# A mixture-of-experts stage in two passes: all first products into one PSUM bank with one bias addition and one Gelu, then all products with the second weights

## The chip, the core and the metric

The kernel runs on one core of a Trainium2 chip. A core has five engines with queues of their own: TensorE (PE in the profile; PEld is its weight load) multiplies matrices and writes into PSUM, VectorE (DVE) and ScalarE (ACT) work on elements, GpSimd (POOL) here only issues gathers, and SyncE (SP) issues nearly all other DMAs. Each queue runs in order: an instruction that waits holds up everything behind it on its engine. PSUM has eight banks of 128 partitions by 512 fp32. The metric is the device time of one execution in microseconds (us), lower is better.

## The reference

Four images of 64 x 64 tokens with 128 channels pass through four layers: deformable attention (layer 0), linear attention (layer 1), an attention and a mixture of experts (layer 2), a causal linear attention and a spectral filter (layer 3). The change touches the experts alone. Cut to them:

```python
def _L2_ffn_ref(x, gate_w, gate_b, weight1, weight2):      # E = 64 experts, K = 8, H = 512, O = 128
    logits = jnp.einsum('bsd,ed->bse', x, gate_w) + gate_b
    probs = jax.nn.softmax(logits, axis=1)
    vals, idx = jax.lax.top_k(probs.transpose(0, 2, 1), K)
    ...
    pooled = jnp.einsum('bked,bke->bed', gathered, topv)
    ones = jnp.ones((E, Bn, 1), dtype=x.dtype)
    h = jnp.concatenate([pooled.transpose(1, 0, 2), ones], axis=-1)
    h = jax.nn.gelu(jnp.einsum('ebd,edh->ebh', h, weight1), approximate=False)
    h = jnp.concatenate([h, ones], axis=-1)
    out = jnp.einsum('ebh,eho->ebo', h, weight2)
    ...
```

For each image every expert gets one pooled token of 128 numbers, multiplies it with its own 128 x 512 matrix, adds a bias, applies Gelu, and multiplies with its own 512 x 128 matrix (the appended one is a second bias). So an image's experts are 64 vector-matrix products of each kind, and 2 x 64 x 256 KB = 33.5 MB of weights, read again for each image.

## The kernel before

All arithmetic is fp32. `hybrid` (line 1733) interleaves two programs. Image b's deformable attention (`Layer0.attend`, line 597) is a loop of 128 steps: four per 128 tokens, one for each of four groups. A step gathers nine samples by nine indirect DMAs on POOL into one of three buffers gt, multiplies them on VectorE with the query (lines 619 to 629), takes the exponential ex on ScalarE (line 633), and forms the weighted sum on VectorE (lines 637 to 645). Beside it run the first stages of image b+1 (`Layer0.front`: the tables from which samples are gathered, lines 428 to 479), and everything that follows for image b-1: `Post.run` (line 808), a generator through layers 1 to 3, of which `layer2_ffn` (line 1029) is one part. Each `yield` of it names a cost; after each attention step `hybrid` advances it until its costs have reached 1176 x (steps done) / 128. When the last image's attention is over, `Post.run` goes through once more alone, with more buffers (`self.wide`).

That is the order in which the program is written. The framework's planner then orders the instructions of each engine's queue itself, by that order as a priority and by when it believes that inputs and buffers are there; so a queue can hold more attention steps beside a stage than the costs say. A buffer of a pool is given again once the readers of its last tile are done.

The experts, in `layer2_ffn` from line 1102, go in 16 groups q of four experts (e = 16 j + q for j from 0 to 3). A group, in order:

- Lines 1112 to 1123: SP loads the four first matrices (w1) and the four second ones (w2), 256 KB each. A tile holds two matrices; the pool has three tiles of each kind beside attention, and ten of each kind in the last, wide run, where the pool is open from the start of `run` (line 811), so that loads can land early.
- Line 1126: four products of one row, ph, for the four experts at partitions 0, 32, 64 and 96 of one bank (one bank beside attention, two wide).
- Line 1131: ScalarE copies the bank to hs. Line 1135: four small products with a matrix that picks these four rows turn hs around into pt, 128 x 16: a hidden unit per partition.
- Line 1140: VectorE adds the bias, g. Line 1143: ScalarE applies Gelu.
- Line 1146: 16 products of g's columns with w2 sum the four experts' outputs into po. After each fourth group line 1153 copies po to os, and line 1156 stores it.

Gelu and the exponential need different tables in ScalarE; a change between them is a table load, an instruction of its own in the trace.

## Time and profile before

| | us |
|---|---|
| time, median of 3 runs (lowest to highest) | 9904.06 (9867.37 to 9940.72) |
| the profiled execution | 9948.3 |
| its span, first to last instruction | 9946.3 |
| attention of images 0 to 3, from about | 273 to 8686 |
| experts of images 0, 1 and 2, beside attention | 2537 to 2850, 4790 to 5096, 7031 to 7299 |
| experts of image 3, alone | 8954 to 9060 |
| mean granted TensorE clock | 0.762 of full speed |

The page of the profile gives, for each engine, its busy time and its instructions, and for each group of instructions the busy time, the mean duration of one, and the idle time of the engine just before it with what ended that. "DVE g L1140 <- PE pt L1135" reads: VectorE stood still before the instruction of line 1140 that writes g, until TensorE's instruction of line 1135 that writes pt was done. "Remote" is a wait whose end the profile can't tie to an instruction. The ends of matrix products are modelled, and some of their records are missing.

The expert stages are where rows of lines 1126 to 1156 stand. Three of the four are beside attention, so a row of theirs can wait for an engine that is busy with another image, and the reverse.

### The profile page before, as it was taken

How to read it: one execution, taken by the hardware profiler on the slowest of the kernel's cores; microseconds unless marked ns; L12 is line 12 of the kernel's file. 1: busy time of each engine (PE TensorE's matmuls, PEld its weight loads, DVE VectorE, ACT ScalarE, POOL GpSimd, SP SyncE). 2: the span in 40 equal slices, each digit the busy share in tenths (PEclk: the TensorE clock that was granted, in tenths of full speed). 3: DMA queues.
4: the chain of work that ended last, by engine and by line, in shares of the span. 5: the costliest groups of instructions: out<-in, count | busy, mean ns of one | idle time of the engine just before them, and what ended most of it. 6: DMA issues, size and time to landing. Idle time of an engine off the chain costs nothing.

```text
span 9946.3 us, 87181 instructions
## 1 busy us (share of the span) xinstructions
PE 5961.9 (60%) x30347; PEld 4144.4 (42%) x30347; DVE 4645.0 (47%) x7777; ACT 2263.7 (23%) x4192; POOL 4400.1 (44%) x4736
## 2 busy tenths in 40 slices
PE   7454100056675777756675667744455667757899
PEld 6242000034344555525344445522234455534676
DVE  1555555565455444466454344456454444443222
ACT  3100000023222222223222222213222222232222
POOL 0665666655434555454534445455535445400000
PEclk9677555567787888877787788866677888877999
DMA  6443333334644444345644444444645444344323
GB/s 211 140 129 109 105 101 105 101 105 142 185 138 142 118 119 121 106 137 150 186 142 141 107 110 119 115 133 140 186 124 147 113 108 116 110 138 127 106 70 81
DMA packets 1131344, 1263.41 MB, mean 127 GB/s; under 512 B 392990, under 2 KB 915481, under 8 KB 1126681
## 3 DMA queue, kind: packets, MB, share of 16 engines
q1 hardware_dynamic: 907309, 652.59, 23.8%
q0 software_dynamic: 221184, 604.27, 21.1%
q8 instruction: 240, 3.93, 0.2%
q14 instruction: 199, 1.63, 0.1%
q10 hardware_dynamic: 2412, 0.98, 0.0%
HBM read 1061.76 MB, written 195.61 MB: 126 GB/s over the span
## 4 chain that ended last, share of the span: by engine, by line
PE 23%; another core or an unknown queue 13%; issue 5%; ACT 5%; DVE 5%; DMA 3%; SPq 1%; POOL 0%; DVEq 0%; ACTq 0%
PE pa L1441 10%; PE pq L1417 4%; ACT y L1431 2%; DMA xin<-x 1%; PE ph L1126 1%; PE pm L428 1%; DVE o L645 1%; PE pt L744 1%; PE pq L874 0%; DVE pr L619 0%; PE pa L1237 0%; PE pn L1247 0%; PE po L1321 0%; PE pt L1135 0%
## 5 line engine op out<-in xcount | busy, mean ns | idle before, releaser
L610 POOL DMA_INDIRECT gt<-tbl,idx x4608 | 4391.2, 953 | 4225.3 <-DVE pv L642 2419.9
L1441 PE MATMUL pa<-y,m 128*128 128x256 f32 x8192 | 2147.1, 415 | 197.6 <-issue 168.1
L1441 PEld LDWEIGHTS pa<-y,m 128*128 128x128 f32 x8192 | 1647.1, 207 | 686.8 <-issue 427.1
L1431 ACT COPY y<-pq 128x1024 f32<-128x1024 f32 x896 | 869.6, 1015 | 2311.6 <-remote 1335.1
L637 DVE TENSOR_TENSOR qa<-cw,ex 128x36 f32<-128x36 f32 x512 | 104.5, 204 | 2212.4 <-ACT ex L633 2066.3
L1417 PE MATMUL pq<-th,xh 32*128 32x256 f32 x8192 | 715.8, 455 | 653.0 <-ACT y L1431 389.1
L645 DVE TENSOR_REDUCE o<-pv 128x32 f32<-128x1152 f32 x512 | 1075.4, 2100 | 21.5 <-remote 10.4
L428 PE MATMUL pm<-wd,xT 128*128 128x256 f32 x2376 | 643.5, 420 | 292.1 <-ACT kv L439 178.3
L1417 PEld LDWEIGHTS pq<-th,xh 32*128 32x128 f32 x8192 | 432.8, 210 | 864.7 <-ACT y L1431 430.6
L619 DVE TENSOR_TENSOR pr<-gt,qa 128x1152 f32<-128x1152 f32 x512 | 689.8, 1347 | 179.3 <-DMA gt<-tbl,idx 151.3
L642 DVE TENSOR_TENSOR pv<-gt,qa 128x1152 f32<-128x1152 f32 x512 | 691.7, 1351 | 70.0 <-remote 25.7
L624 DVE TENSOR_REDUCE s<-pr 128x36 f32<-128x1152 f32 x512 | 687.4, 1343 | 1.8 <-DVE sc L627 1.2
L428 PEld LDWEIGHTS pm<-wd,xT 128*128 128x128 f32 x2376 | 485.2, 211 | 421.8 <-ACT kv L439 198.2
L633 ACT ACTIVATE ex<-sc,mx 128x9 f32<-128x9 f32 x512 | 157.0, 307 | 1131.4 <-DVE mx L629 504.4
L461 PE MATMUL pm<-xT,wd 128*128 128x512 f32 x576 | 309.6, 686 | 171.7 <-ACT qo L478 125.5
L1428 DVE COPY y<-pq 128x1024 f32<-128x1024 f32 x128 | 156.8, 1225 | 466.2 <-ACT y L1431 466.2
L579 PE MATMUL qa<-sident,qt 128*128 128x128 f32 x256 | 52.0, 336 | 437.7 <-issue 266.5
L1126 PE MATMUL ph<-w,pooled 128*1 128x512 f32 x512 | 234.1, 800 | 47.9 <-DMA w<-in_L_ffn_weight_dram 30.5
L461 PEld LDWEIGHTS pm<-xT,wd 128*128 128x128 f32 x576 | 120.1, 220 | 336.8 <-issue 185.2
L661 PE MATMUL pt<-ident,o 128*128 128x128 f32 x128 | 33.5, 353 | 355.2 <-issue 253.9
L147 ACT ACTIVATE ln<-xin,ln,ln 128x128 f32<-128x128 f32 x512 | 212.3, 483 | 122.1 <-DMA xin<-x 88.6
L579 PEld LDWEIGHTS qa<-sident,qt 128*128 128x128 f32 x256 | 44.7, 235 | 454.2 <-issue 276.0
(377 smaller groups left out, 6399.4 us busy)
## 6 DMA issues: line engine op xcount, KB each, us to landing
w<-in_L_ffn_weight_dram SPq DMA_DIRECT2D x512, 256.0 KB
th<-th SPq DMA_DIRECT2D x512, 256.0 KB
gt<-tbl,idx POOLq DMA_INDIRECT x4608
xin<-x SPq DMA_DIRECT2D x224, 256.0 KB
x<-xin SPq DMA_DIRECT2D x160, 256.0 KB
tbl<-kv SPq DMA_DIRECT2D x264, 128.0 KB
th<-wx SPq DMA_DIRECT2D x32, 1024.0 KB
q<-qd SPq DMA_DIRECT2D x288, 64.0 KB
```

What stands on the lines that cost most here:

```text
L147: self.nc.scalar.activation(dst, src, AF.Identity, bias=self.shift[:, i : i + 1], scale=self.rstd[:, i : i + 1])
L428: nc.tensor.matmul(pm[:, t, :], lhsT=self.xf[:, at : at + P], rhs=self.wd[:, tap, C:], start=(t == 0 and tap == 0), stop=False,)
L461: nc.tensor.matmul(pv, lhsT=self.wd[:, tap, :C], rhs=self.xT[:, 8 * c + dy : 8 * c + dy + 8, dx : dx + HW], start=(tap == 0), stop=False,)
L610: nc.gpsimd.indirect_dma_start(out=gt[:, i, :], out_offset=None, in_=self.tbl[b % 2][:, :], in_offset=bass.IndirectOffsetOnAxis(ap=blk.idx ...
L619: nc.vector.tensor_mul(pr, corners[:, :, 0:32], qa[:, q0 + 32 * g : q0 + 32 * g + 32].unsqueeze(1).to_broadcast([P, 4 * K2, 32]),)
L624: nc.vector.tensor_reduce(s4, pr, AX.X, ALU.add)
L642: nc.vector.tensor_mul(pv, corners[:, :, 32:64], aw.unsqueeze(2).to_broadcast([P, 4 * K2, 32]),)
L645: nc.vector.tensor_reduce(o[:, t, 32 * g : 32 * g + 32], pv.rearrange("p i s -> p s i"), AX.X, ALU.add)
L1126: nc.tensor.matmul(ph[32 * j : 32 * j + 1, :], lhsT=pooled[:, 16 * j + q : 16 * j + q + 1], rhs=w1s[j], start=True, stop=True,)
L1417: nc.tensor.matmul(pq[:, r // 2, r % 2, :, pair, :], lhsT=xh[rows, 2 * (q % 4) + pair, :], rhs=t[rows, 2 * (q % 2) + pair, :].rearrange("p ...
L1431: nc.scalar.copy(to, src)
L1441: nc.tensor.matmul(pa[:, h * 2 * P : (h + 1) * 2 * P].rearrange("p (g x) -> p g x", g=8), lhsT=s.m[u][:, KC * kc + i, :], rhs=yv[:, i], st ...
```

## The change

The groups run in two passes. The first takes all 16 groups as far as pt, which becomes one tile for all of them: 16 columns a group, 256 in all, in one bank. Then one addition adds all biases, and one Gelu is applied. The second pass makes the products with the second weights, and copies and stores as before. Both kinds of weights come from tiles of one tag, w: six of them beside attention and 20 in the wide run, the same bytes as before. The copy os now uses the two buffers of hs. Each pass yields 2.5 sixteen times, where one loop yielded 5.0 sixteen times.

```diff
@@ run
-            self.ws = self.pool(ctx, "fwx", 10) if self.wide else None
+            self.ws = self.pool(ctx, "fwx", 20) if self.wide else None
@@ layer2_ffn
-                ws = self.ws or self.pool(ectx, "fws", 3)
+                ws = self.ws or self.pool(ectx, "fws", 6)
                 wk = self.pool(ectx, "few", 2)
...
+                pt = ps.tile([P, 512], F32, tag="p", name="pt")
+                ptv = pt[:, : 4 * E].rearrange("p (q c j) -> p q c j", c=4, j=4)
+
+                def first(e):
+                    return self.a["L2_ffn_weight1"][e, :C, :]
+
+                def second(e):
+                    return self.a["L2_ffn_weight2"][e, :FH, :].rearrange("(c p) o -> p c o", p=P)
+
+                def weights(q, src):
+
+                    got = []
+                    for j in range(4):
+                        if j % 2 == 0:
+                            t = ws.tile([P, 2, FH], F32, tag="w", name="w")
+                        to = t[:, j % 2]
+                        if src is second:
+                            to = to.rearrange("p (c o) -> p c o", c=4)
+                        nc.sync.dma_start(to, src(16 * j + q))
+                        got.append(t[:, j % 2])
+                    return got
+
                 for q in range(16):
-                    w1s, w2s = [], []
-                    for j in range(4):
-                        e = 16 * j + q
-                        if j % 2 == 0:
-                            w1 = ws.tile([P, 2, FH], F32, tag="w1", name="w1")
-                            w2 = ws.tile([P, 2, 4, C], F32, tag="w2", name="w2")
-                        nc.sync.dma_start(w1[:, j % 2], self.a["L2_ffn_weight1"][e, :C, :])
-                        nc.sync.dma_start(
-                            w2[:, j % 2],
-                            self.a["L2_ffn_weight2"][e, :FH, :].rearrange("(c p) o -> p c o", p=P),
-                        )
-                        w1s.append(w1[:, j % 2])
-                        w2s.append(w2[:, j % 2])
+                    w1s = weights(q, first)
                     ph = phs[q % len(phs)]
...
                     hs = wk.tile([P, FH], F32, tag="hs", name="hs")
                     nc.scalar.copy(hs, ph)
-                    pt = ps.tile([P, 512], F32, tag="p", name="pt")
-                    ptv = pt[:, :16].rearrange("p (c j) -> p c j", c=4)
                     for c in range(4):
                         nc.tensor.matmul(
-                            ptv[:, c, :], lhsT=hs[:, c * P : (c + 1) * P], rhs=w.pick,
+                            ptv[:, q, c, :], lhsT=hs[:, c * P : (c + 1) * P], rhs=w.pick,
                             start=True, stop=True,
                         )
-                    g = wk.tile([P, 4, 4], F32, tag="g", name="g")
-                    nc.vector.tensor_add(
-                        g, ptv, w.b1T.rearrange("p c (j q) -> p q c j", j=4)[:, q]
-                    )
-                    nc.scalar.activation(g, g, AF.Gelu)
+                    yield 2.5
+                g = wk.tile([P, 16, 4, 4], F32, tag="g", name="g", bufs=1)
+                nc.vector.tensor_add(g, ptv, w.b1T.rearrange("p c (j q) -> p q c j", j=4))
+                nc.scalar.activation(g, g, AF.Gelu)
+                for q in range(16):
+                    w2s = weights(q, second)
                     for c in range(4):
                         for j in range(4):
                             nc.tensor.matmul(
                                 po[32 * j : 32 * j + 1, (q % 4) * C : (q % 4 + 1) * C],
-                                lhsT=g[:, c, j : j + 1], rhs=w2s[j][:, c, :],
+                                lhsT=g[:, q, c, j : j + 1], rhs=w2s[j][:, c * C : (c + 1) * C],
                                 start=(c == 0), stop=(c == 3),
                             )
                     if q % 4 == 3:
-                        os = wk.tile([P, 4, C], F32, tag="os", name="os", bufs=1)
+                        os = wk.tile([P, 4, C], F32, tag="hs", name="os")
                         nc.scalar.copy(os.rearrange("p q c -> p (q c)"), po)
...
-                    yield 5.0
+                    yield 2.5
```

## The prediction

> **What bounds the kernel now.** I read the page first (busy times, then the chain of waits), then busy times by stretch, then the waits inside the three stretches in which image b's experts run beside image b+1's attention, then the order of time inside one of them.
>
> ```profile
> PE 5961.9 (60%) x30347; PEld 4144.4 (42%) x30347; DVE 4645.0 (47%) x7777; ACT 2263.7 (23%) x4192; POOL 4400.1 (44%) x4736
> ...
> PE 23%; another core or an unknown queue 13%; issue 5%; ACT 5%; DVE 5%; DMA 3%; SPq 1%; POOL 0%; DVEq 0%; ACTq 0%
> ```
>
> No engine is full: the kernel is bound by engines that wait for each other. The changed lines run four times. These stretches, in order, are attention beside little else (the yardstick), the three expert stages beside attention, and the last one alone ("wide"):
>
> ```profile
> core 0: us, PE busy (x) PEld busy (x) DVE busy (x) ACT busy (x) POOL busy (x), PEclk, DMA share, GB/s
> 1160.00:1960.00 800.00, 59.56 (x178) 37.04 (x178) 442.39 (x605) 37.78 (x153) 540.97 (x570) 0.52 0.35 103
> 2537.00:2850.00 313.00, 198.97 (x1051) 92.35 (x1050) 136.09 (x202) 67.53 (x122) 157.41 (x166) 0.77 0.62 190
> 4790.00:5096.00 306.00, 195.66 (x984) 86.54 (x985) 131.26 (x192) 58.21 (x109) 148.77 (x158) 0.74 0.61 187
> 7031.00:7299.00 268.00, 132.96 (x820) 55.18 (x819) 115.44 (x176) 55.31 (x100) 136.61 (x146) 0.66 0.66 203
> 8954.00:9060.00 106.00, 81.38 (x770) 38.74 (x769) 3.30 (x17) 17.95 (x39) 0.00 (x0) 0.73 0.73 219
> ```
>
> Counted by line 642 (one product per group of nine samples), the yardstick holds 63 attention steps in 800 us, 12.7 us each. The expert stages hold 19, 18 and 16 steps, which alone would take 241, 229 and 203 us. So the experts cost 72, 77 and 65 us more than the attention that they run beside: 214 us in all is the most that hiding them fully could save there. DMA is not full: its share makes 194, 187 and 177 us of busy time, under the attention's own time.
>
> Where the 214 us go, first stage:
>
> ```profile
> POOL gt L610 <- DVE pv L642: 119.8, 13, 18.0
> ACT hs L1131 <- remote: 92.4, 6, 23.4
> DVE g L1140 <- PE pt L1135: 84.6, 11, 19.1
> ...
> DVE g L1140 <- remote: 43.1, 3, 23.8
> DVE qa L637 <- ACT ex L633: 37.2, 10, 17.4
> ```
>
> and SP's own waits, between its DMA issues:
>
> ```profile
> SPq L1118 <- remote: 88.8, 4, 23.8
> SPq L1118 <- PE po L1146: 46.9, 7, 9.4
> ```
>
> VectorE stands still before the bias addition g (with short ones, 131, 118 and 112 us in the three stages) and ScalarE before the copy hs (121, 105, 105 us). Both carry attention too: what stands behind them waits, the gather buffers are not freed, and POOL stops. One of the long ones:
>
> ```profile
> 7243.01 1.05 PE L1126 MATMUL ph<-w,pooled 128*1 128x512 f32 x3 [0.22 <-issue]
> ...
> 7252.22 0.95 POOL L610 DMA_INDIRECT gt<-tbl,idx  x1 [0.30 <-issue]
> 7256.49 1.48 SPq L1118 DMA_DIRECT2D w<-in_L_ffn_weight_dram  x3
> 7256.70 0.59 ACT L1131 COPY hs<-ph 128x512 f32<-128x512 f32 x1 [16.14 <-remote]
> ...
> 7259.24 0.18 DVE L1140 TENSOR_TENSOR g<-pt,b1T 128x16 f32<-128x16 f32 x1 [13.84 <-PE pt L1135]
> ```
>
> The product ends at about 7244, yet its reader and SP's next load start at 7256.5, some 3.3 us after POOL's last gather. TensorE's word arrives late while POOL streams gathers ("remote" in these rows). So each handover from TensorE to an engine that attention needs can cost up to some 20 us.
>
> **The change, part by part.** Durations are of the profiled execution: 9948.3 us, its span of 9946.3 plus 2.0 around it. The median shown is 9904.06, 0.44% less; I carry the sum over as a ratio.
>
> *Removed: additions and Gelus.* Per stage 16 additions of 0.176 us and 16 Gelus of 0.216 become one of each on 256 columns. Nearest rows: line 1176 adds 512 columns in 0.69 us, line 1131 copies 512 in 0.59; so about 0.4 us each. The busy time saved, some 5 us a stage, lies beside waits: nothing counted. What counts is the wait: 16 handovers from TensorE to VectorE become one.
>
> *Removed: table loads.* Gelu and attention's Exp displace each other: 14, 12 and 12 loads before Gelu and 13, 12 and 12 before Exp, 75 of 1.283 us, 96 us of ScalarE. Those before Exp stand in VectorE's path (line 637 waits for ex); the others lie partly beside products. The Trainium skill, "ScalarE: Activation LUTs", section "What ACT_TABLE_LOAD costs", puts a switch at about 2.66 us, as it adds a drain to the load. In this trace Gelu starts 0.01 us after its load ends (7239.05 plus 1.28, Gelu at 7240.34), so I use 1.283: 37 loads before Exp are 47 us, by the page they would be 98.
>
> *Moved: second products, and their weights.* All 512 products with the second weights (rows of 0.27 to 0.42 us, four side by side) go behind the last first product. In pass two nothing of VectorE waits for an expert, and ScalarE only for four copies os. I give pass two half of the stage, so 107 of the 214 us, and let 85% go: 91 us. The rest stays for os and for TensorE's waits for weights.
>
> *Pass one.* It keeps its 16 copies hs, each waiting for TensorE, on the engine that also has to issue ex: what the additions no longer hold, these can hold. Of its 107 us I take off the Exp loads of its half, 24 us, and 20 more for the vanished additions. The ends are 0 (hs holds all that g held) and 80 (the waits of g go and none is replaced); I stay near the low end because hs waited 331 us in sum already, g 361, largely at the same time.
>
> *Added: the border.* The addition waits for the last of 16 groups, then Gelu, then the first second product. One ordinary handover is about 2 us; a held one, by the row at 7256, 16 us more. I take 8 us a stage, 24 in all. Meanwhile six tiles of second weights load, which covers the start of pass two. Here the Trainium skill speaks against the change: "Perfetto Trace Analysis", section "Matmuls" under "Optimizing Tensor Performance", wants independent products to rotate through PSUM banks so that reading one overlaps the next, and the change stops doing that for pt. By the rule the emptying is exposed; by the rows it is one addition of 0.4 us instead of 16 waits summing to over 110 us a stage. I follow the rows; the rule's cost is inside the 24.
>
> *Weights on SP.* Still 128 DMAs of 256 KB a stage at about 0.50 and 0.43 us of issue, 60 us; none added. They are reordered: 64 of the first kind, then 64 of the second, six shared tiles in place of three and three. A load now waits for the product three half-steps before, no longer for the second product at the end of the chain (SP waited 136 us for that in the first stage). Behind a waiting load on SP stand attention's query loads and the table stores of the next image: they gain with it. POOL's queue is passed by nothing. TensorE now meets a load's wait in both passes (7, 23 and 50 us in one today); with the same bytes I count no change, 0 to 15 us a stage either way. The copy os shares hs's two buffers in place of one of its own: nothing, as hs is idle then; without that cover, four waits of a 2 KB store, a few us.
>
> *The wide stage.* 106 us hold 81 us of TensorE and 0.73 x 106 = 77 us of DMA. TensorE idles 20 us before products of these lines. Without the round trip by ScalarE, VectorE and ScalarE in each group it should come to 81 plus some 12 at the two ends: 12 us off (0 to 25).
>
> Sum: 91 + 24 + 20 - 24 + 12 = 123 us; 9948.3 becomes 9825, a ratio of 0.9876, and the median 9904 becomes 9782. Nothing takes the gain back later: what follows on each queue just starts sooner.
>
> **Rivals.** *The wait moves to ScalarE.* Attention's ex queues behind hs. For it: hs already waits longest for "remote", and pass one meets twice as many copies per attention step. Against it: pass two has none. Then pass one loses more than before, pass two gives 91, and what is left is some 40 us: 9865, no change.
>
> *Fewer attention steps beside the experts (slower).* The planner fixes each queue's order. By pacing, a stage of cost 80 at 1176/128 = 9.19 a step should pass 8.7 attention steps; the trace has 16 to 19, because the chain of waits kept the experts behind. If the plan now sees a short chain, about 9 steps remain beside them. The stage is then DMA's: 33.5 MB at 219/0.73 = 300 GB/s is 112 us, gathers 9 x 0.35 x 12.7 = 40, other transfers some 15, so 167 us at a full share. Attention alone needs 114. At a share of 0.70 the stage takes 239 us, 125 over attention where it was 72: 160 us more in three stages, about 10050. It decides below a share of 0.76 (219 us); the stages have 0.61 to 0.66 now, the best 50 us of the first 0.80. Against it: bytes and products per stage are unchanged, and these may be what stretched the plan.
>
> *It does not do what it says.* The last stage could lose its early loads: 40 weight DMAs land before it today, and must remain 40 (20 tiles) or it gains nothing.
>
> **How the numbers follow.** The main case has 0.47, the wait on ScalarE 0.32, fewer steps 0.21. About 1% is what a measurement here can tell from no change. The main case reaches from 70 us off to all 214 plus 25, six sevenths of it beyond 1% (0.40); of the second some 0.04 is beyond 1% and the rest within; the third is slower by over 1% in 0.19. So faster 0.44, same 0.36, slower 0.20. The range takes the main case's best (239 us off, 9670) and goes up to 9960, into the third case, whose worse half is left out.
>
> **What would show it.** Right: table loads before line 1143's successor fall from 39 to about 4; VectorE waits for g once a stage; the three stages hold as many attention steps at some 15 us each in pass one and 13 in pass two; the wide stage is near 94 us. Wrong: ex waits grow on line 637 by 100 us or more (first rival); the stages hold about 9 attention steps at a DMA share of 0.7 (second).

## The result and the profile after

| | before | after |
|---|---|---|
| time, median of 20 runs each, us | 9890.12 | 9921.44 |
| lowest to highest, us | 9841.64 to 9940.72 | 9884.64 to 9999.92 |
| ratio of after to before, 95% interval | | 1.0045 (1.0031 to 1.0059) |

The change makes the kernel 0.45% slower. The prediction was 9782 us, 1.2% faster than the median it started from. The profiled execution of after has a span of 9910.1 us; that of before, with 9946.3, took 58 us more than its own median. So the two spans can't be set against each other as wholes. Stretches inside them can, with some 10 to 20 us of scatter in each: the three stages beside attention took 308, 300 and 267 us from first product to end in this trace of the old loop, and 319, 284 and 264 in that of a later run that has the old loop there.

The busy times on the page of after:

```profile
PE 5962.5 (60%) x30347; PEld 4124.3 (42%) x30347; DVE 4637.3 (47%) x7717; ACT 2157.8 (22%) x4062; POOL 4395.0 (44%) x4736
```

Busy time fell as foreseen: ScalarE by 106 us and 130 instructions. Waiting took its place. Next the same kind of table as in the prediction, by stretch: first and second pass of each of the four stages, the last stage being the two rows at the end. The first pass ends with the addition g. A stage ends, here and in the prediction, with the addition of the experts' output oe (line 1162 before, 1172 after), 5 to 30 us behind its last product.

```profile
core 0: us, PE busy (x) PEld busy (x) DVE busy (x) ACT busy (x) POOL busy (x), PEclk, DMA share, GB/s
2516.00:2668.00 152.00, 124.22 (x448) 57.92 (x447) 63.97 (x96) 20.45 (x51) 76.58 (x81) 0.83 0.65 205
2668.00:2854.00 186.00, 92.36 (x614) 36.42 (x614) 82.80 (x106) 10.96 (x35) 97.27 (x103) 0.69 0.60 169
4774.00:4901.00 127.00, 100.35 (x370) 45.77 (x370) 60.05 (x89) 16.25 (x41) 60.47 (x64) 0.78 0.66 213
4901.00:5093.00 192.00, 100.73 (x615) 37.94 (x615) 83.24 (x109) 10.74 (x35) 105.05 (x113) 0.69 0.61 173
6994.00:7124.00 130.00, 69.02 (x270) 31.79 (x268) 58.24 (x90) 14.53 (x37) 71.75 (x76) 0.57 0.70 227
7124.00:7277.00 153.00, 64.69 (x545) 24.93 (x545) 71.56 (x94) 9.47 (x30) 84.17 (x90) 0.54 0.63 182
8887.00:8958.00 71.00, 58.75 (x258) 29.24 (x257) 0.67 (x2) 10.86 (x18) 0.00 (x0) 0.52 0.55 167
8958.00:9019.00 61.00, 38.88 (x512) 17.13 (x512) 0.42 (x2) 4.04 (x6) 0.00 (x0) 0.58 0.74 188
```

The stages beside attention take 338, 319 and 283 us where they took 313, 306 and 268, and hold 21, 20 and 18 attention steps where they held 19, 18 and 16. The last one takes 132 where it took 106. Beside attention the second pass, which was to run free there, is the longer of the two each time.

The waits inside the first stage, longest first:

```profile
DVE qa L637 <- ACT ex L633: 149.8, 14, 26.8
POOL gt L610 <- DVE pv L642: 118.8, 12, 16.1
PEld po L1156 <- issue: 88.2, 59, 4.1
ACT os L1163 <- PE po L1156: 83.1, 3, 32.7
PE po L1156 <- issue: 59.4, 38, 3.1
```

VectorE's wait for g (131 us here before) is down to 10. Attention's wait for the exponential (line 637) has grown from 37 to 150 us in its place, and POOL stops as long as before: 118.8 against 119.8 us. In the other two stages line 637 shows the same, before (first two rows) and after:

```profile
DVE qa L637 <- ACT ex L633: 45.5, 9, 17.5
DVE qa L637 <- ACT ex L633: 18.0, 8, 7.6
DVE qa L637 <- ACT ex L633: 152.8, 13, 29.5
DVE qa L637 <- ACT ex L633: 123.8, 10, 24.7
```

With short and unnamed waits taken in, VectorE stood 361 us before g and 113 before line 637 in the three stages of the kernel before; now it stands 20 and 454. That is 474 us both times (for 53 and 59 attention steps): the wait has moved as a whole. On ScalarE the waits before hs stayed (331 and 315 us), and those before os grew from 110 to 295.

The other rows of the first stage were small before: ScalarE before the copy os, and TensorE before second products for "issue", so for nothing that the profile shows (7 us before the products and 19 before their weight loads in this stage). Over the whole kernel, from the groups of instructions (busy and mean, then the idle time before them):

```profile
L1156 PE MATMUL po<-w,g 128*1 128x128 f32 x2048 | 184.6, 358 | 264.7 <-issue 200.6 <-ACT os L1163 32.9 <-DMA w<-in_L_ffn_weight_dram 25.2
L637 DVE TENSOR_TENSOR qa<-cw,ex 128x36 f32<-128x36 f32 x512 | 104.5, 204 | 2515.2 <-ACT ex L633 2344.6 <-issue 121.5 <-ACT hs L1142 14.8
L633 ACT ACT_TABLE_LOAD x19 | 24.4, 1283 | 14.1 <-issue 8.2 <-DVE sc L627 3.1 <-DVE s L624 2.5
L1163 ACT COPY os<-po 128x512 f32<-128x512 f32 x16 | 9.4, 585 | 348.4 <-PE po L1156 313.5 <-remote 34.9
```

In the kernel before:

```profile
L637 DVE TENSOR_TENSOR qa<-cw,ex 128x36 f32<-128x36 f32 x512 | 104.5, 204 | 2212.4 <-ACT ex L633 2066.3 <-issue 128.2 <-ACT kv L439 9.4
L1153 ACT COPY os<-po 128x512 f32<-128x512 f32 x16 | 9.4, 585 | 117.2 <-remote 77.4 <-PE pm L472 11.4 <-PE pm L433 9.4
```

There the second products waited 46.9 us in all, and line 633 had 56 table loads.

What the new "issue" looks like, in the order of time in the second pass of the first stage:

```profile
2718.31 1.15 PE L472 MATMUL pm<-ind,vb 128*128 128x64 f32 x4
...
2726.26 0.08 PEld L1156 LDWEIGHTS po<-w,g 128*1 128x1 f32 x1 [2.72 <-issue]
2726.55 0.95 POOL L610 DMA_INDIRECT gt<-tbl,idx  x1 [0.30 <-issue]
2727.66 0.37 PE L1156 MATMUL po<-w,g 128*1 128x128 f32 x1 [2.43 <-issue]
...
2733.97 0.59 ACT L478 COPY qo<-pm 128x512 f32<-128x512 f32 x1 [19.03 <-remote]
...
```

While POOL streams gathers without a pause, a weight load and its product follow each other at 1.4 us, though each takes 0.08 and 0.37. Meanwhile ScalarE stands 19 us before the copy qo, with attention's ex behind it (it starts at 2734.46). The products that qo reads had ended at 2719.5, 14.5 us before, so it is TensorE's word that is late, as in the prediction's row at 7256, and not its work.

### The profile page after: what moved, and what is told of

Read it like the earlier page. It is cut to its first block, busy times and chain, and to the rows that moved or that the text cites. A ratio compares the mean times of both kernels' runs of the same rounds, so it can differ in the third digit from the quotient of the medians.

```text
span 9910.1 us, 86932 instructions
## 1 busy us (share of the span) xinstructions
PE 5962.5 (60%) x30347; PEld 4124.3 (42%) x30347; DVE 4637.3 (47%) x7717; ACT 2157.8 (22%) x4062; POOL 4395.0 (44%) x4736
## 4 chain that ended last, share of the span: by engine, by line
PE 34%; another core or an unknown queue 20%; issue 13%; DVE 8%; ACT 7%; POOL 5%; DMA 4%; SPq 1%; DVEq 0%; ACTq 0%; POOLq 0%
PE pa L1451 13%; PE pq L1427 5%; POOL gt L610 5%; ACT y L1441 4%; PE pm L428 1%; PE pm L461 1%; DVE o L645 1%; PE ph L1137 1%; DMA xin<-x 1%; PE po L1156 1%; DVE pr L619 1%; DVE s L624 1%; PE pq L874 1%; DMA gt<-tbl,idx 1%
## 5 line engine op out<-in xcount | busy, mean ns | idle before, releaser
L637 DVE TENSOR_TENSOR qa<-cw,ex 128x36 f32<-128x36 f32 x512 | 104.5, 204 | 2515.2 <-ACT ex L633 2344.6
L1156 PE MATMUL po<-w,g 128*1 128x128 f32 x2048 | 184.6, 358 | 264.7 <-issue 200.6
L1156 PEld LDWEIGHTS po<-w,g 128*1 128x1 f32 x2048 | 73.2, 99 | 397.4 <-issue 288.8
```

The costliest lines, as they stand in the source:

```text
L1156: nc.tensor.matmul(po[32 * j : 32 * j + 1, (q % 4) * C : (q % 4 + 1) * C], lhsT=g[:, q, c, j : j + 1], rhs=w2s[j][:, c * C : (c + 1) * C], ...
```

## Which stages lose

Two runs put the change into some of the stages only; both keep the two versions of the loop in one kernel. The second has the condition the other way round.

```diff
@@ layer2_ffn, two passes beside attention only
+                if self.wide:
                     ws = self.ws or self.pool(ectx, "fws", 3)
...
+                else:
+                    ws = self.ws or self.pool(ectx, "fws", 6)
...
```

> Two passes in the three stages beside attention, the old single loop in the last stage alone. Theory A (the loss sits in the last stage, which took 132 us where it took 106): with the old loop there it takes 106 again, and the ratio to the kernel before falls from 1.0045 to about 1.001 (0.999 to 1.003). Theory B (the loss sits beside attention, where copies os and hs hold the exponentials on ScalarE): the ratio stays at 1.003 to 1.006.

Measured: 1.0008 (0.999 to 1.0026). Its last stage took 103 us.

> The old loop in the three stages beside attention, two passes in the last stage alone. Theory A (the last stage carries the loss): last stage about 132 us, ratio about 1.0027 (26 us of 9890). Theory B (the loss is beside attention): ratio within 1.0000 to 1.001.

Measured: 1.0022 (1.0006 to 1.0038), with a last stage of 132 us. So the last stage, which runs once and alone, carries the loss, as far as the runs can place it (theory A), and in the three stages beside attention, where the prediction saw 111 us of gain, no gain shows. Two things are to be explained: a loss of about 25 us there, and a gain that did not come here.

## The last stage: a store at the head of the line

Two causes suggest themselves in the row of its first pass: a clock of 0.52, and a DMA share of 0.55 (both 0.73 over the whole stage before). In its second half the order of time shows SP's queue like this:

```profile
8937.13 0.37 SPq L1129 DMA_DIRECT2D w<-in_L_ffn_weight_dram  x1
8965.51 1.15 SPq L1166 DMA_DIRECT2D oe<-os  x4
8966.70 13.12 SPq L1129 DMA_DIRECT2D w<-in_L_ffn_weight_dram  x16
```

and SP's waits in the stage:

```profile
SPq L1166 <- ACT os L1163: 38.7, 4, 27.9
```

Nothing was issued for 27.9 us. SP had come to the store of the first four groups, whose products can start only when the whole first pass is through. In the loop before, that store came after four of sixteen groups, while there were others to compute; there too SP waited before the four stores, but 25.5 us in all and at most 10.9 at once. Behind the store stand loads of second weights whose tiles are free already. They start when the second pass has begun, and TensorE then waits for them. Four runs test this.

First the rival, the clock. The first products of the next group are placed ahead of each copy hs, so that TensorE has work during it (old loop beside attention).

```diff
+                    ahead = [products(q) for q in range(len(phs) - 1)]
                     for q in range(16):
+                        if q + len(phs) - 1 < 16:
+                            ahead.append(products(q + len(phs) - 1))
                         hs = wk.tile([P, FH], F32, tag="hs", name="hs")
-                        nc.scalar.copy(hs, ph)
+                        nc.scalar.copy(hs, ahead[q])
```

> As the run with two passes in the last stage alone, but in its first pass the first products of group q+1 stand in the program ahead of the turned-around copy of group q, so that TensorE has work while ScalarE copies hs. Theory C (the last stage is slow because TensorE stands still 0.77 us in every group of 4.45 us and so keeps its low granted clock, 0.50 in most of the pass): the granted clock of the first pass rises above 0.75, the pass goes from 71 us to about 45, the stage to some 105 to 112, and the ratio to 1.000. Rival D (the stage is bound by its weights: 88 loads of 256 KB after its start, the second ones late): the first pass may shorten, the second lengthens by as much, the stage stays above 125 us, and the ratio at about 1.0027.

Measured: 1.0009 (0.9989 to 1.0029). The two passes of the stage in this run:

```profile
8889.00:8949.00 60.00, 57.56 (x248) 29.94 (x240) 0.00 (x0) 10.63 (x17) 0.00 (x0) 0.50 0.63 197
8949.00:9011.00 62.00, 38.68 (x513) 16.86 (x513) 0.58 (x1) 4.04 (x6) 0.00 (x0) 0.56 0.70 184
```

From its first product to the addition g the pass takes 62 us in place of 70, as TensorE no longer waits 0.7 us in each group. But its clock stays at 0.50 while TensorE is busy 57.6 of 60 us: theory C's reason for the low clock falls, the standing still. What the low clock costs this run can't tell, as it did not rise. The second pass gains nothing, as the store stands where it stood.

Next the stores on ScalarE's queue, behind the copy that they store, and in another run four banks for po, with copies and stores behind all second products.

```diff
@@ stores on ScalarE
-                            nc.sync.dma_start(
+                            nc.scalar.dma_start(
                                 self.oe[e : e + 4, :].rearrange("(u q) c -> u q c", u=1),
@@ four banks
+                pos = [po] + [p.tile([P, 512], F32, tag="p", name="po") for p in (ps_h, ps, ps)]
+                for t in pos[1:]:
+                    nc.vector.memset(t, 0.0)
...
-                    if q % 4 == 3:
+                for q in range(3, 16, 4):
                     os = wk.tile([P, 4, C], F32, tag="hs", name="os")
-                    nc.scalar.copy(os.rearrange("p q c -> p (q c)"), po)
+                    nc.scalar.copy(os.rearrange("p q c -> p (q c)"), pos[q // 4])
```

> Two passes everywhere, but the sixteen small stores of os stand on ScalarE's queue, directly behind the copy that they store, in place of SP's. Theory E (in the last stage SP stands 27.9 us before the first store, with the loads of the later second weights behind it, so that the second pass has to wait for them): with the store off SP's queue the DMA share in the second half of the first pass is no longer near zero, the second pass goes from 61 us to about 30 to 35, the last stage from 132 us to some 100 to 106, and the ratio falls from 1.0045 by about 0.003 to 1.001. Rival D (the 88 loads take that long whatever stands between them): the last stage stays above 125 us and the ratio at 1.003 to 1.006. For the stages beside attention: if SP's waits before the stores also held weights there, the ratio falls below 1.000.

Measured: 1.0003 (0.9989 to 1.0017). The stage took 124 us, not 100 to 106: with the store gone from SP's queue, a load there waited for the store's landing all the same, by the profile.

```profile
SPq L1129 <- DMA oe<-os: 24.0, 1, 24.0
```

The run speaks for theory E only in part: its second pass took 54 us in place of 61, where 30 to 35 were expected. The run with four banks tells more.

> Two passes everywhere, but the second pass writes its four quarters into four banks, and the four copies os stand behind all of its products. Theory B1 (in the second pass the copies os hold attention's exponentials on ScalarE while they wait for po, 313 us in 14 waits): these waits fall below 120 us, VectorE's wait for ex at line 637 falls by 100 us or more from 2345, and the ratio falls from 1.0045 to 1.000 or less. Rival B2 (the copies only show that TensorE issues the 512 second products slowly while POOL streams gathers; attention loses nothing by them): the ratio stays at 1.003 to 1.006 and the stages keep their length.

Measured: 0.9983 (0.997 to 0.9995). SP's queue in its last stage, and the two passes:

```profile
8935.85 56.11 SPq L1129 DMA_DIRECT2D w<-in_L_ffn_weight_dram  x53
8992.05 7.39 SPq L1170 DMA_DIRECT2D oe<-os  x16
```

```profile
8898.00:8968.00 70.00, 57.98 (x255) 28.73 (x256) 1.94 (x4) 10.87 (x18) 0.00 (x0) 0.52 0.76 230
8968.00:8998.00 30.00, 21.83 (x514) 14.15 (x514) 0.58 (x1) 2.45 (x5) 0.00 (x0) 0.90 0.90 238
```

All 53 loads go out in one row. The second pass takes 30 us to its last product, 34 to its end in place of 61, and the stage 104 us. The first pass is as slow as it was. So theory E holds: without the store among the loads the 26 us are gone. That does not clear the clock. The second pass runs at 0.90 here, where it ran at 0.58 while it waited for weights; and the first pass stays at about 0.5, with TensorE busy 58 of 70 us. The old loop, too, gains when its stores leave SP's queue (93 us in place of 106, further down), so two passes keep some 10 us of loss there. Both together (four banks, first products ahead, also beside attention with a second bank):

> Four banks and late copies as in the run of that kind (ratio 0.9983), and in the first pass the first products of a group stand one group ahead of the copy hs, with two banks for them beside attention too. If the waits of hs for ph (174 us from products, 110 remote there) still hold attention's exponentials, they fall by half and the ratio goes to 0.995 or less; in the last stage the first pass loses 11 us (71 to 60). If what is left is not those waits, only the last stage gains: 0.997 to 0.998.

Measured: 0.994 (0.9922 to 0.9959). The last stage took 96 us, with a DMA share of 0.88 and 0.87. That is some 36 us less than in the changed kernel; the ratio fell by more (1.0045 to 0.994, some 100 us). By the trace, another 27 us went between the experts' start and the point at which attention goes on behind them (the next part has this measure). The waits of hs fell from 374 to 328 us in sum, not by half, so the expected cause isn't shown, and where the rest comes from stays open.

## Beside attention: what ate the gain

**The second products.** The run with four banks also tested whether the copies os hold attention. Their waits fell from 348 to 171 us in sum. Yet line 637's wait for ex fell by 56 us only (2344.6 to 2288.2), not by 100: in the second pass of the first stage ScalarE now stood 60.4 us before the next image's copy qo, which waits for TensorE too. Theory B1 is not shown. What all these waits have behind them is TensorE, which is late. Two runs take instructions away from it. One leaves out half of the second products (`for c in range(2)`). The other multiplies four columns of g with four experts' weights at once, and stores of the result only the blocks in which column and expert belong together:

```diff
-                        for j in range(4):
-                            nc.tensor.matmul(
-                                po[32 * j : 32 * j + 1, (q % 4) * C : (q % 4 + 1) * C],
-                                lhsT=g[:, q, c, j : j + 1], rhs=w2s[j][:, c * C : (c + 1) * C],
+                        nc.tensor.matmul(
+                            po[32 * (q % 4) : 32 * (q % 4) + 4, :].rearrange("p (j c) -> p j c", j=4),
+                            lhsT=g[:, q, c, :], rhs=w2[:, :, c * C : (c + 1) * C],
```

> Two passes everywhere, with only half of the second products (hidden units 0 to 255; the other half is left out, all weights are still loaded). Theory F (TensorE's slow issue of the 512 second products while POOL streams gathers sets the length of the second pass beside attention: 325 us of gaps in the whole kernel, 265 of them before products of po): second passes of 186, 192 and 153 us become some 35 us shorter each, and the ratio falls from 1.0045 to 0.995 or less. Rival G (attention's own steps set the second pass: 12 steps of 12.7 us are 152): the passes shorten by less than 15 us each, and the ratio stays above 1.000.

> Two passes, but a weight tile holds four matrices (3 tiles beside attention, 10 in the last stage: the same bytes), and one product per chunk multiplies the four columns of g of a group with the four experts' second weights side by side: 64 second products of 512 columns a stage in place of 256 of 128 columns, and only the diagonal blocks are stored. Theory F (the second pass is slow by the number of instructions, about 0.7 us each while POOL streams): a quarter of the instructions, so the gaps before second products fall from 265 us on the page to under 80, the second passes become some 30 us shorter each, as with half of the products, ratio 0.999 or less. Rival (the products' own time counts): 128 records of 0.6 to 1.0 us one behind the other are 80 to 130 us of TensorE a stage where it was 40; the second passes get no shorter, ratio 1.004 or more.

Measured: 0.9989 (0.9971 to 1.0008) and 0.9979 (0.9964 to 0.9994). The first row is that of the second products in the second run:

```profile
L1155 PE MATMUL po<-w,g 128*4 128x512 f32 x512 | 244.7, 688 | 129.4 <-issue 65.5 <-DMA w<-in_L_ffn_weight_dram 33.3 <-ACT os L1162 27.6
```

TensorE is busy 60 us longer with them, and the last stage is some 17 us longer. Yet the second passes beside attention, from the addition g to that of oe, take 157, 156 and 130 us in place of 186, 191 and 153. With half of the products they take 169, 173 and 137. (In the run with two passes beside attention alone they took 182, 178 and 152; so the sums, 443 and 478 us against 530 and 513, say more than a single pass.) About as much arrived in the time: 65 and 55 us, by ratios of 0.9979 and 0.9989 against 1.0045. So the second pass shortens with fewer instructions, with half of the work in one run and with more work in the other, which speaks for theory F: their number stretches it, not their work. That is not quite proof, as the tile of four matrices moves the loads too and its stores have another form, and the run with half of the products has neither change but less work. And the sizes were missed: with half of the products a pass became 17 us shorter, not 35, and the ratio is not 0.995 or less; with one product for four the idle time before second products is 129 us, not under 80.

**The 55th step.** Attention's steps can be counted by line 642. Image 2 has two rows here: its steps up to a gap, and that gap. First the kernel before:

```profile
core 0: us, DVE busy (x), PEclk, DMA share, GB/s
4228.00:5147.00 919.00, 72.81 (x54) 0.74 0.56 161
5147.00:5263.00 116.00, 0.00 (x0) 0.95 0.21 63
```

then after:

```profile
4218.00:5096.00 878.00, 72.84 (x54) 0.74 0.56 160
5096.00:5250.00 154.00, 0.00 (x0) 0.87 0.32 94
```

Behind the experts come the addition of their output and layer 3's attention, and these have their place in the queues after the 54th attention step of the next image, in both kernels. When attention comes there early, it stands still until they are done. So time won beside the experts is won only if the experts end earlier too. From the first expert product to the end of this gap, the three images take 483, 469 and 445 us before, 1398 in all, and 486, 473 and 443 after, 1401. (Two other runs with the old loop beside attention have 1393 and 1391, the one with two passes there 1394.) The two more steps that pass in each stage are missing behind it: between the steps at its two ends the gap is 158, 157 and 140 us where it was 152, 119 and 128.

Two runs raise the cost that the experts' yields name, in each kernel (here the changed one; in the kernel before 5.0 becomes 10.0), so that more attention steps come first.

```diff
-                    yield 2.5
+                    yield 5.0
...
-WORK = 1176.0
+WORK = 1256.0
```

> The changed kernel, with the sixteen and sixteen yields of the two passes at a cost of 5.0 in place of 2.5 and the total at 1256 in place of 1176, so that some five more attention steps stand ahead of layer 3's attention. Theory H (attention is held at a fixed step, the 55th of each image, until layer 3's attention is through, and so gives back there whatever it gained beside the experts: the gap behind the experts was 158, 157 and 140 us where it was 152, 119 and 128, and from the first expert product to the end of that gap both kernels take the same 1400 us in sum): the step at which it is held moves to about 59, the gaps fall by 30 us or more each, and the ratio falls from 1.0045 to 1.000 or less. Rival I (the gap is layer 3's own work, which attention can't run beside): the gaps keep their length, ratio 1.003 to 1.006.

> The kernel before with the same change of costs (its sixteen yields at 10.0 in place of 5.0, the total at 1256). Theory H: its gaps shrink too, but it has less to give back (two attention steps fewer in each expert stage), so it gains less than the changed kernel does: ratio 0.998 to 1.000. Rival I: ratio within 0.999 to 1.002 and gaps as before.

Measured: 0.9985 (0.9967 to 1.0004) and 0.9921 (0.9903 to 0.994). Image 2 in the kernel before with the new costs:

```profile
4189.00:5151.00 962.00, 79.56 (x59) 0.77 0.56 163
5151.00:5217.00 66.00, 0.00 (x0) 0.92 0.22 65
```

Attention is held at the 60th step in place of the 55th, in both, and the gaps fall to 111, 105 and 76 us (after) and 77, 71 and 56 (before). Theory H is right on the place, and rival I falls. But H also said that the changed kernel has more to give back and would gain more, and it does not: with the new costs it is 0.64% slower than the kernel before with them, on one chip, where it was 0.45% slower. So the held step is where time won beside the experts goes; but when it is moved, two passes are still the slower version.

**Stores in the kernel before.** SP's stores of os hold weights in the old loop too.

> The kernel before, with the same move of its sixteen stores from SP to ScalarE. It tells whether what the store costs is the change's own. In the kernel before, SP waited 54 us before these stores in the second and third stage and next to nothing in the last. Theory E: the store stands among the loads of its own group there, two groups of loads are ahead of it, so the move gains little: ratio 0.998 to 1.001, last stage within 5 us of 106. Rival (any store on SP costs the stages): ratio below 0.997.

Measured: 0.9927 (0.99 to 0.9955): the rival was right. The last stage took 93 us, and the gaps fell to 104, 95 and 80 us. The expectation had SP wait next to nothing before the stores of the last stage; the trace of before has the 25.5 us named above.

## Two kinds of chip

The runs so far were made on chips where the kernel before takes about 9900 us. The next seven fell on two chips where it takes about 7830. Each chip on record was used at one time only, and these two last; so the difference could also go with the time of the runs, and "kind of chip" is short for both. Three leave the indices out of the gathers, to see what TensorE's slow issue goes with:

```diff
-                nc.gpsimd.indirect_dma_start(
-                    out=gt[:, i, :], out_offset=None, in_=self.tbl[b % 2][:, :],
...
+                nc.gpsimd.dma_start(
+                    gt[:, i, :], bass.AP(
+                        self.tbl[b % 2].tensor, self.tbl[b % 2].offset + col * P * P,
+                        [[P, P], [1, 256]],
+                    ),
```

> The changed kernel with each gather of 128 table rows replaced by a plain copy of 128 neighbouring table rows of the same size, still issued by POOL: attention's samples are then other numbers, the bytes and the number of POOL's DMAs are the same. It tells what TensorE's slow issue of second products goes with. Theory J1 (with POOL's issue of DMAs of any kind): gaps of about 0.7 us between second products stay, their idle time before po near the 265 us on the page, second passes near 186, 192 and 153 us. J2 (with gathers by index alone): the gaps fall below 80 us. J3 (with the traffic of attention's samples): as J1.

> The same plain copies, issued by SP, so that POOL is silent: same bytes. J1 and J2 (POOL's issuing is what it goes with): the gaps before second products fall below 80 us in sum, and ScalarE's waits named remote before hs and os go too. J3 (the traffic): the gaps stay near 265 us.

> The run with plain copies issued by POOL (attention's samples are other numbers) once more. On a chip where the kernel before takes about 9900 us: if the gaps between second products go with POOL's issuing or the traffic, they stay above 200 us; if they go with gathers by index, they fall below 80 us.

Measured: 7075.71, 7160.76 and 7085.42 us. They can't answer: on these chips the slow issue hardly shows, with gathers or without (25 and 33 us before second products' weight loads in the two kinds with plain copies). That was found by the two kernels, unedited:

> The kernel before once more, with nothing edited, for its profile on the same chip as the run of the changed kernel. From the first expert product to the end of the gap behind the experts, summed over three images, it should again take within 20 us of 1395, if its chip is one of those with 9900 us.

> The changed kernel once more, with nothing edited, as a second profile beside the one before: on the chip of the runs with plain copies the kernel before took 7831 us, not 9900, and its descendants showed almost none of TensorE's gaps. Theory F2 (the gaps between second products belong to the chips on which the kernel before takes 9900 us): on such a chip the idle time by issue before second products is again above 200 us and the ratio 1.003 to 1.006; on a chip where the kernel before takes about 7830 us it is below 40 us, and if the gaps were what ate the gain, the ratio is below 0.995; if the last stage and ScalarE's waits ate it, the ratio is 1.000 or more there too.

Measured: 0.9999 (0.999 to 1.0008) for the kernel before, and 1.0112 (1.0097 to 1.0127) for the changed one, 7910 against 7823 us. The change costs more here than on the other chips. Groups of the kernel before on this chip:

```profile
L637 DVE TENSOR_TENSOR qa<-cw,ex 128x36 f32<-128x36 f32 x512 | 105.0, 205 | 553.2 <-ACT ex L633 549.6 <-issue 2.1
L1131 ACT COPY hs<-ph 128x512 f32<-128x512 f32 x64 | 37.4, 585 | 210.0 <-PE ph L1126 209.9
```

and of the changed kernel:

```profile
L1156 PE MATMUL po<-w,g 128*1 128x128 f32 x2048 | 139.3, 350 | 87.6 <-DMA w<-in_L_ffn_weight_dram 52.7 <-ACT os L1163 30.0 <-ACT g L1151 4.8
L637 DVE TENSOR_TENSOR qa<-cw,ex 128x36 f32<-128x36 f32 x512 | 105.1, 205 | 540.8 <-ACT ex L633 538.7 <-issue 0.7
```

No "remote" before hs, next to no "issue" before second products (35 us before their weight loads, where it was 289), and line 637 waits 550 us for ex where it waited 2066. With TensorE's word in time, there is less for the change to win: in the three stages beside attention VectorE waited 96 us for g before, not 361. By stretch, the first stage up to its last product and what follows it up to the end of the gap, here with the steps of line 642 alone; before:

```profile
2134.00:2332.00 198.00, 22.98 (x17) 0.89 0.94 289
2332.00:2507.00 175.00, 5.39 (x4) 0.89 0.39 110
```

after:

```profile
2132.00:2346.00 214.00, 25.30 (x19) 0.90 0.92 277
2346.00:2521.00 175.00, 4.06 (x3) 0.87 0.35 103
```

From the experts' last product to the gap's end both take 175 us, so the stage's own length is what counts, and DMA is nearly full in it: a share of 0.94 and 0.92. VectorE's wait for its gathers to land shows what that does, in the first stage (up to its end) before and after:

```profile
DVE pr L619 <- DMA gt<-tbl,idx: 13.1, 5, 6.9
DVE pr L619 <- DMA gt<-tbl,idx: 51.5, 15, 8.1
```

In the three stages it grew from 46 to 155 us, more than the 88 us by which the wait for g fell (96 to 8). So here the wait moved to DMA, not to ScalarE. Two more attention steps beside the experts bring their own gathers, 128 x 9 rows of 1 KB a step, so 2.4 MB for two, which is 8 us at 289 GB/s. The stage is 16 us longer; the other half is not settled, though SP stood 23.5 us before stores in its second pass. (In the third image the part behind the stage grew too, from 171 to 187 us.) In the three images, from the first attention step of image 1 to the last of image 3, this makes 4904 us in place of 4847; behind the last attention step 1283 in place of 1252. That is 57 + 31 = 88 us, the measured 87.

Two more kernels take the aids found so far together. The first is the kernel before with stores on ScalarE and the new costs. The second has these too, with two passes and one product for four experts beside attention, and the old loop in the last stage.

> The kernel before with both things that the runs showed to help it: its stores of os on ScalarE's queue (ratio 0.9927 alone) and the costs that hold attention at a later step (0.9921 alone). If the two act on different waits, their gains add up: 0.984 to 0.987, last stage 88 us. If both only shorten the same gap behind the experts: 0.989 to 0.992.

> Two passes beside attention with one product for the four experts of a group (ratio 0.9979 as it was), stores on ScalarE, costs as in the run of the kernel before, and the old loop with its stores on ScalarE in the last stage. If two passes are worth having once TensorE's instructions are few, this is faster than the kernel before with the same two aids: below 0.984. If the waits of ScalarE for TensorE beside attention remain what counts, it stays behind that kernel: 0.986 to 0.992.

Measured: 0.9806 (0.9787 to 0.9825) and 0.9875 (0.9856 to 0.9893), against the kernel before on the same chip. The best version on these chips is the single loop with those two edits. It was not run on a chip of the other kind, where each edit alone gave 0.993 and 0.992.

## Why the prediction was wrong

- **"I give pass two half of the stage, so 107 of the 214 us, and let 85% go: 91 us."** The step that failed first. By the same measure, time over 12.7 us a step, pass one has 38 + 25 + 28 = 91 us left and pass two, with 12, 12 and 10 steps, 34 + 40 + 26 = 100. So pass two gave 7 us in place of 91, and pass one 16 in place of 44. The prediction left 16 us of pass two for the four copies os and TensorE's waits for weights. But each copy waits on ScalarE for the products of four groups from an engine whose word is late, with attention's ex behind it: their wait went from 110 to 295 us in the three stages. And the second products come in one row while POOL gathers; they waited 47 us in all before and 265 after. (The 512 that the prediction counts a stage are 256 products with two records each.)
- **"Nothing takes the gain back later."** Wrong. The 23 us by which the stages are better in that measure (214 less 191) went into the wait at the 55th step; the block up to its end takes 1401 us where it took 1398. The excess over attention was the wrong currency: the work that ends the block is the chain from the experts through layer 3. The gap behind the stages is there in the trace of before, and the prediction has no term for it.
- **"The copy os shares hs's two buffers ...: nothing, as hs is idle then; without that cover, four waits of a 2 KB store, a few us."** The third step. The store was asked only whether its buffer is free, not how long it waits at the head of SP's queue: 27.9 us, with loads behind it. The trace of before showed the place: 25.5 us of SP's waits before these stores in the last stage. So "12 us off" for the last stage became 26 us on.
- **Table loads.** Right: 39 to 4 before Gelu and 56 to 19 before the exponential, 35 and 37 fewer, where 38 and 37 were counted, at 1.283 us each.
- **The border.** Right: one wait of VectorE for g a stage, 90 us in all, of which 70 lie in the last stage, where VectorE has nothing else to do, and 20 beside attention. From the end of the last first product to the first second one 5.1, 4.5, 5.3 and 3.8 us pass, where 8 a stage were foreseen. So the exposed emptying of a bank, which the Trainium skill ("Perfetto Trace Analysis", section "Matmuls" under "Optimizing Tensor Performance") would avoid by rotating banks, comes to 15 us beside attention with all that belongs to the border, inside the 24.
- **The rivals.** The first names what happened beside attention: the wait moved to ScalarE, 474 us of VectorE's waits as before, and line 637's grew by over 100 us (278 in the whole kernel). It put this on hs in pass one and saw none in pass two; in the first stage pass two has 85 of the 150 us, before os and qo. Its time of 9865 was 0.4% below before's 9904, the result 0.45% above. The second is refuted: no stage held fewer steps. The third did not come about: 40 loads of weights were issued at 8668 to 8699 us, before the last stage, as in the kernel before. That 9921 us lies inside the range up to 9960 is luck: the range reached there for the second rival, which did not happen, and the loss in the last stage had no place in it.

Set against the sum: 23 us in place of the 111 beside attention, nothing of it left behind the gap, and 26 lost in place of 12 won. That makes some 26 us slower, where the medians differ by 31 and the ratio says 44.

The ratios of different groups of runs come from different chips with times near 9900 us, so differences between groups of 0.2% are not read.

What stays open: what makes TensorE's issue and word late on one kind of chip, how much of the lost gain there each of os, qo and the product count has by itself, and what the low clock of the last first pass costs.

## What to carry to other kernels

Splitting a loop into two passes moves its stores to the end of the second pass: look at what is queued behind them, above all loads for a buffer that is already free. Find what ends the block, and where the faster engine will be held next, before time "over attention" is counted as time saved. Add up all waits of the engine that is to be freed, before and after: a wait that is gone from one line can stand whole on another. And count instructions, not only their durations, for an engine that a whole pass leans on.

## What the hardware showed beside

On the chips with 9900 us, an attention step behind the gap takes 16.4 us (1197 us for 73); on those with 7830, 11.4 (831 for 73), with POOL's gathers at 0.95 us on both. The difference is in waits. ScalarE stands 1335 us for "remote" before the copies y of line 1431 in the kernel before on the one, and not at all on the other; the products pa of line 1441 wait 168 us for "issue" on the one, and not at all on the other.

TensorE's granted clock does not follow its busy time alone. In the first pass of the last stage it stayed at 0.50 with TensorE busy 57.6 of 60 us, in products of 512 columns with one output row and products of four columns. In the second pass of the run with four banks it was 0.90 at 22 of 30 us busy, in products of 128 columns, again with one output row. What decides is not shown here.
